# Post-norm decoder layer on one core: where in the queue the next block's feed-forward reads are issued

## The chip, the cores and the metric

The kernel runs on one core of one Trainium2 chip. The metric is device time in microseconds (us) of one execution; lower is better. A run's time includes a little that lies outside the profiled span of instructions.

The core has five engines that run side by side, each on its own stream of instructions: TensorE (PE: matmuls; its weight loads are shown apart as PEld), VectorE (DVE), ScalarE (ACT), GpSimd (POOL) and SyncE (SP), which in this kernel does nothing but issue transfers (DMAs). Transfers issued by SP, ACT or POOL are carried out by the core's 16 DMA engines.

## What is computed

The reference is one decoder layer on 8 sequences of 256 tokens, 512 wide, in float32. Cut to what matters:

```python
def reference(x, ctx_2048, Wq, Wk, Wv, Wo, Wdown, Wup, decay, gate_cp, up_cp, down_cp):
    x = layernorm(x + attention(x, ...))           # 16 heads of 32
    x = layernorm(x + xattn(x, ctx, ctx, decay))   # a decayed running sum of ctx*ctx, times x
    x = layernorm(x + ffn(x, gate_cp, up_cp, down_cp))

def ffn(h, gate_cp, up_cp, down_cp):
    gate_w = spline_reconstruct(gate_cp, 2048, 512)
    up_w   = spline_reconstruct(up_cp, 2048, 512)
    down_w = spline_reconstruct(down_cp, 512, 2048)
    inter = silu(h @ gate_w.T) * (h @ up_w.T)
    return inter @ down_w.T
```

`spline_reconstruct` makes each weight matrix by cubic interpolation of a line of control points, some 129 weights to a point. So along a row of a weight matrix the values are one cubic polynomial for a long stretch, and the kernel never builds the full matrices.

## The kernel before

**Attention and the second norm** come first, in four groups of 512 tokens, and fill the span up to about 402 us. They leave the layer's middle result in the tile `x2`.

**The feed-forward** works on four blocks `b` of 512 tokens (loop at line 939). Because a weight row is piecewise cubic, a product with it needs only two things of a token: some samples of its features near the places where the cubic changes, and a few moments (sums against fixed polynomials) for the rest. For block `b` these stand in one tile, `xgs[b]` (name `xg`, two buffers): in each half of its partitions 44 rows of samples and 20 rows of moments, for 8 places.

`inputs(b)` (line 700) makes that tile, as a generator of eight steps which `fill(n)` advances:

- Steps 1 to 4, one for each chunk `c` of 128 features: PE transposes the chunk of `x2`, ACT or DVE copies it from PSUM to the tile `xt`, and two transfers write it to a scratch tensor `xd` in device memory, in an order in which rows that are read together are near each other: the bulk from POOL's queue (line 713), and for `c` above 0 a few left-over rows from SP's queue (line 716).
- Step 5: `windows` (line 683) is called. It issues, on SP, one small write of the left-over rows of chunk 0 into `xd` (line 687) and then four reads of samples from `xd` into `xg` (line 692), two of 88 KB and two of 616 KB.
- Steps 5 to 8: PE makes the moments, DVE and ACT copy them out, POOL's queue writes them to the scratch tensor `md`, and `moments` (line 694) issues two reads of 320 KB on SP, from `md` into `xg`.

For blocks 0 and 1 (`b > 1` is false at lines 718 and 743) `inputs` runs during the last group of attention and the reads are issued at once. For blocks 2 and 3 the two calls are put into the list `reads`. `inputs(2)` is advanced in block 1 and `inputs(3)` in block 2: four steps ahead of the block's loop (line 942), the other four after the third pair (line 950).

**One block's main loop** (line 943) goes over eight pairs `j`. `gate_up` makes two tiles of 128 gate and up products from `xgs[b]`, applies silu and multiplies them into two tiles `inter`. `gather` (line 858) issues for each of them one transfer of 256 KB on SP, which regroups the rows into the tile `nat` (two halves: the first eight gatherings fill one, the last eight the other). So a block has 16 gatherings.

After the loop, block by block: the list `reads` is emptied, which issues its reads behind the 16 gatherings; then PE makes the products `y` with `exact(b, t)`, `t` from 0 to 15, four matmuls each, one for each quarter of the outputs. In this loop `slot()` advances the chains of the preceding block's third norm, whose results go out as four writes `out` on SP. At `t == 7`, `into_sums` (line 875) makes four sums `ps_s` from both halves of `nat`; each is copied out and written by SP into the tile `fin` (line 892). After `t == 15`, `finish` (line 894) adds the products of `fin` to `y`.

The order of work is written out by hand: the class `Ordered` keeps every engine's instructions in the order of the program, and since it records all operations through one helper, nearly all carry line 308 in the profile. An engine takes its instructions strictly in that order, SP among them: while SP's next transfer waits for its data, everything after it on SP waits as well. The transfers of SP share a ring of eight semaphores, used in turn.

Of the kernel before, what the change touches and what calls it, by code (L numbers as in the profile page):

```python
# [18 lines left out]
B, T, D = 8, 256, 512  # L19
# [9 lines left out]
ND = 4  # L29
# [5 lines left out]
STEP, SPAN = 8, 129  # L35
# [280 lines left out]
def decoder_kernel(ctx: ExitStack, tc: tile.TileContext, x, xT, ctxT, wq, wkT, wvT, woT, wdownT, wup, decay, up_taps, down_taps, mom_f, sum_f, out, plan):  # L316
    nc = tc.nc
# [27 lines left out]
    nc = Ordered(tc)  # L345
    units, chains = [], []

    def slot():

        for c in list(chains):  # L350
            if next(c, c) is c:
                chains.remove(c)

    def fill(n):

        for i in range(n):
            if units:
                next(units[0][1])
                units[0][2] -= 1
                if not units[0][2]:  # L360
                    units.pop(0)
            if i % 2:
                slot()
                some_taps()
# [76 lines left out]
    def some_taps():  # L441
        made[0] += 0.62
        while made[0] >= 1:
            made[0] -= 1
            next(weights, None)
# [235 lines left out]
    xgs, reads = {}, []  # L681

    def windows(xd, xt, xg):


        past = SPAN * ND - D
        nc.sync.dma_start(out=xd[4 * (SPAN - past) + 3 :: 4, :], in_=xt[:past, 0, :])
        for h, odd, n, j0 in ((0, 0, NTILE // 2 - 1, 1), (1, NTILE - 1, NTILE // 2 - 1, 0)):
            for t, m, j in ((odd, 1, odd // 2), (2 * j0 + h, n, j0)):
                step = 4 * (lows[t + 2][0] - lows[t][0]) if m > 1 else 0  # L690
                from_ = bass.AP(xd.tensor, xd.offset + 4 * lows[t][0] * GT, [[GT, RAW], [step * GT, m], [1, GT]])
                nc.sync.dma_start(out=xg[h * K2 : h * K2 + RAW, j : j + m, :], in_=from_)

    def moments(md, xg):
        for h in range(2):
            to = h * K2 + RAW
            from_ = bass.AP(md.tensor, md.offset + h * GT, [[NTILE * GT, 20], [2 * GT, NTILE // 2], [1, GT]])
            nc.sync.dma_start(out=xg[to : to + 20], in_=from_)

    def inputs(b):  # L700

        pool, mf = ffn["pool"], ffn["mf"]
        xt = pool.tile([P, DC, GT], F32, tag="x2T", name="x2T")
        xd = ffn["dram"].tile([4 * SPAN, GT], F32, tag="xd", name="xd")
        md = ffn["dram"].tile([1, 20 * NTILE, GT], F32, tag="md", name="md")
        xg = pool.tile([P, NTILE // 2, GT], F32, tag="xg", name="xg", bufs=2)
        xgs[b] = xg
        for c in range(DC):
            tr = ps_mm.tile([P, GT], F32, tag="mm", name="tr_x2")
            for t in range(TC):  # L710
                nc.tensor.transpose(tr[:, t * P : (t + 1) * P], x2[:, b * TC + t, c * P : (c + 1) * P], ident)
            (nc.vector.tensor_copy if c % 2 else nc.scalar.copy)(xt[:, c, :], tr)
            nc.gpsimd.dma_start(out=xd[c : 4 * (P - 1 - c) + c + 1 : 4, :], in_=xt[c:, c, :])
            if c:
                row = 4 * (SPAN - c) + c - 1
                nc.sync.dma_start(out=xd[row : row + 4 * c - 3 : 4, :], in_=xt[:c, c, :])
            yield
        if b > 1:
            reads.append(lambda: windows(xd, xt, xg))
        else:  # L720
            windows(xd, xt, xg)
        mo = ffn["mom"].tile([P, ND, GT], F32, tag="fin", name="mom")
        ps = {}
        for c in range(DC):
            for s in (c, c + 1):
                if s // 2 not in ps:
                    ps[s // 2] = ps_mm.tile([P, GT], F32, tag="mm", name="ps_mom")
                at = slice(s % 2 * K2, (s % 2 + 1) * K2)
                nc.tensor.matmul(
                    ps[s // 2][at, :],  # L730
                    lhsT=mf[:, c, s - c, :],
                    rhs=xt[:, c, :],
                    start=(s == c + 1 or c == 0),
                    stop=(s == c or c == DC - 1),
                )
            if c == 1:
                nc.vector.tensor_copy(mo[:, 0, :], ps[0])
            if c == DC - 1:
                nc.vector.tensor_copy(mo[:, 1, :], ps[1])
                nc.scalar.copy(mo[:K2, 2, :], ps[2][:K2, :])  # L740
                nc.gpsimd.dma_start(out=md[:, : 2 * P].rearrange("h (c p) t -> (h p) c t", p=P), in_=mo[:, :2, :])
                nc.gpsimd.dma_start(out=md[0, 2 * P :], in_=mo[:K2, 2, :])
                if b > 1:
                    reads.append(lambda: moments(md, xg))
                else:
                    moments(md, xg)
            yield
# [94 lines left out]
    def gate_up(b, j):  # L842

        pgs, pus = [], []
        for w, pool, tag, to in ((wg, ps_mm, "mm", pgs), (wu, ps_big, "big", pus)):
            for h in range(2):
                at = slice(h * K2, (h + 1) * K2)
                ps = pool.tile([P, GT], F32, tag=tag, name="pg" if w is wg else "pu")
                nc.tensor.matmul(ps, lhsT=w[at, j * P : (j + 1) * P], rhs=xgs[b][at, j, :], start=True, stop=True)
                to.append(ps)  # L850
        for h in range(2):
            sg = work.tile([P, GT], F32, tag="sg", name="sg")
            nc.scalar.activation(sg, pgs[h], AF.Silu)
            inter = work.tile([P, GT], F32, tag="inter", name="inter", bufs=NTILE)
            nc.vector.tensor_tensor(inter, pus[h], sg, ALU.mult)
            inters[b, 2 * j + h] = inter

    def gather(b, t):

        g, r = t // NSUM, t % NSUM  # L860
        if not r:
            nats[b, g] = work.tile([P, NSUM, GT], F32, tag=f"nat{g}", name="nat", bufs=1)
        nc.sync.dma_start(out=nats[b, g][r::NSUM], in_=inters[b, t])

    def exact(b, t):

        if t == 0:
            ys[b] = [ps_big.tile([P, GT], F32, tag="big", name=f"y{d}") for d in range(ND)]
        for d in range(ND):
            q = slice(d * 32, (d + 1) * 32)  # L870
            nc.tensor.matmul(
                ys[b][d], lhsT=wd[q, t * P : (t + 1) * P], rhs=inters[b, t][q, :], start=(t == 0), stop=False
            )
# [33 lines left out]
    def outcome(b, t):  # L907

        tr = ps_mm.tile([P, D], F32, tag="mm", name="tr_y")
        for d in range(ND):  # L910
            nc.tensor.transpose(tr[:, d * P : (d + 1) * P], ys[b][:, d, t * P : (t + 1) * P], ident)
        yield
        h3 = rows.tile([P, D], F32, tag="row", name="h3")
        s3 = small.tile([P, 1], F32, tag="s3", name="s3")
        nc.vector.scalar_tensor_tensor(h3, tr, 1.0, xps[b][:, t, :], ALU.mult, ALU.add, accum_out=s3)
        yield from norm_plain(h3, s3, h3, tr)
        r0 = (b * TC + t) * P
        nc.sync.dma_start(out=out[r0 : r0 + P, :], in_=h3)
# [16 lines left out]
    def settle():  # L935
        while chains:
            slot()

    for b in range(NG):
        if 0 < b < NG - 1:  # L940
            units.append(["i", inputs(b + 1), 2 * DC])
            fill(DC)
        for j in range(NTILE // 2):
            gate_up(b, j)
            gather(b, 2 * j)
            gather(b, 2 * j + 1)
            if b:
                slot()
            if b and j == 2:
                fill(DC)  # L950
        if b == 0:
            fill(2 * DC)
        while reads:
            reads.pop(0)()
        for t in range(NTILE):
            exact(b, t)
            if b and t == 0:
                chains += [outcome(b - 1, c) for c in range(TC)]
            slot()
            if b == 0 and t < 5:  # L960
                slot()
            if b == 0 and t == 4:
                settle()
                done.close()
                late = ffn["mom"] = ctx.enter_context(tc.tile_pool(name="late", bufs=1, side="right"))
            if t == 7:
                settle()
                chains.append(residual(b))
                for v in range(NSUM // 2):
                    into_sums(b, v)  # L970
        assert not units
        finish(b)
# [54 lines left out]
```

## Time and profile before

| | us |
|---|---|
| median of three runs | 616.04 (615.62 to 616.34) |
| profiled execution | 616.05 |
| its span, first to last instruction | 614.3 |
| PE busy (matmuls) | 582.3 (95%) |
| DVE / ACT / POOL busy | 334.7 / 277.7 / 210.6 |
| feed-forward, block 1: start of the next block's transposes, to the same in block 2 | 449.86 to 505.42 |
| the same, block 2 (to the first product of block 3) | 505.42 to 561.00 |
| mean granted clock of PE | 0.986 |

Times in the feed-forward are given from the start of the span. The profile's page divides the span into 40 slices and gives busy shares in tenths; "PEclk" is the granted clock of PE in tenths. In lists of instructions a group such as `xg<-xd` names what is written and what is read. "SPq" marks transfers by the time of their issue on SP; when a transfer lands is told by its semaphore's events in the trace. In a table of stretches the columns are: the stretch, its length, the busy time of PE, PEld, DVE, ACT and POOL (with the number of instructions), then the granted clock, the mean busy share of the 16 DMA engines, and GB/s. That share can come out over 1 because packets of one engine overlap. Float32 matmuls appear as two instructions each.

### The profile page before, as it was taken

Reading aid. Unit: us, or ns where it says so; the run is one execution under the profiler, and the core shown is the slowest. Engines: PE = TensorE matmul, PEld = TensorE weight load, DVE = VectorE, ACT = ScalarE, POOL = GpSimd, SP = SyncE. Lnnn points to the kernel's source line nnn. Section 1 sums busy time; section 2 is a strip of 40 time slices with the busy share of each in tenths; the row PEclk is TensorE's granted clock in tenths of the full one; section 3 lists DMA queues with packets and bytes.
Section 4 is the critical chain, followed back from the end, with each engine's and each line's share of the span. In section 5 each row is a group of like instructions: output and inputs, shape, how many; then the busy total and the mean of one; then the engine's idle time right before and its main releaser. Section 6 shows DMA issues by size and latency. Waiting matters only on the chain.

```text
span 614.3 us, 9693 instructions
## 1 busy us (share of the span) xinstructions
PE 582.3 (95%) x3346; PEld 293.8 (48%) x3346; DVE 334.7 (54%) x742; ACT 277.7 (45%) x820; POOL 210.6 (34%) x479
## 2 busy tenths in 40 slices
PE   8999999998999999999999998999999969988994
PEld 3544555555455546555546554544344334433432
DVE  0203545657875656785656778777446216503714
ACT  0115634647555447555446666563135115303502
POOL 0001986264635434635321202202611602430152
PEclk9999999999999999999999999999999979997998
DMA  8104263044224115314102654687159839982941
GB/s 286 65 0 154 85 191 104 1 138 137 56 66 138 41 47 181 112 52 138 35 18 61 187 123 126 155 200 147 71 138 229 190 104 234 197 221 59 212 151 68
DMA packets 39984, 75.50 MB, mean 123 GB/s; under 512 B 3936, under 2 KB 8288, under 8 KB 39936
## 3 DMA queue, kind: packets, MB, share of 16 engines
q1 hardware_dynamic: 36880, 66.94, 40.7%
q0 software_dynamic: 2048, 6.77, 3.4%
q10 hardware_dynamic: 1008, 1.18, 0.6%
q8 instruction: 26, 0.43, 0.3%
q14 instruction: 22, 0.18, 0.1%
HBM read 42.86 MB, written 11.04 MB: 88 GB/s over the span
## 4 chain that ended last, share of the span: by engine, by line
PE 74%; DVE 10%; DMA 9%; ACT 3%; issue 2%; SPq 1%; POOLq 0%; POOL 0%; DVEq 0%; ACTq 0%
PE ps_k L308 9%; PE ps_v L308 9%; PE y L308 8%; PE ps_o L308 8%; PE ps_q L308 7%; PE tr_e L308 6%; PE sc L308 5%; PE pg L308 5%; PE av L308 5%; DMA xg<-md 4%; PE pu L308 4%; DVE nmax L308 3%; DMA xd<-x2T 2%; PE ps_s L308 2%; PE ps_mom L308 2%; ACT e L308 2%
## 5 line engine op out<-in xcount | busy, mean ns | idle before, releaser
L308 ACT ACTIVATE e<-sc,nmax 128x256 f32<-128x256 f32 x256 | 120.0, 480 | 101.1 <-DVE nmax L308 101.1
L308 DVE TENSOR_REDUCE nmax<-sc 128x2 f32<-128x512 f32 x128 | 84.5, 682 | 73.5 <-PE sc L308 67.5
L308 POOL TENSOR_TENSOR taps<-taps 128x256 f32<-128x256 f32 (+1 forms) x144 | 88.5, 614 | 32.9 <-DMA taps<-in_down_taps 25.7
L308 PEld LDWEIGHTS tr_e<-ident,e 128*128 128x128 f32 x512 | 56.9, 140 | 25.2 <-issue 22.5
L308 PE MATMUL tr_e<-ident,e 128*128 128x128 f32 x512 | 68.3, 276 | 0.5 <-DVE eT L308 0.4
L308 PE MATMUL y<-inter,wd 32*128 32x512 f32 x512 | 63.1, 598 | 0.0
L308 POOL TENSOR_SCALAR va<-ss 128x1 f32<-128x1 f32 x32 | 7.3, 227 | 162.1 <-ACT x L308 85.8
L308 PE MATMUL ps_o<-w_o,yT 128*128 128x512 f32 x128 | 60.0, 600 | 1.6 <-DVE eT L308 1.2
L308 PE MATMUL ps_k<-xT_g,w_k 128*128 128x512 f32 x128 | 58.8, 600 | 0.7 <-DVE eT L308 0.5
L308 PE MATMUL ps_v<-w_v,xT_g 128*128 128x512 f32 x128 | 58.6, 598 | 0.4 <-DVE eT L308 0.4
L308 PE MATMUL ps_q<-xT_g,w_q 128*128 128x512 f32 x128 | 58.3, 596 | 0.0
L308 ACT ACTIVATION_READ_ACCUMULATOR e<-sc,nmax 128x1 f32 x256 | 53.2, 208 | 0.0
L308 POOL TENSOR_TENSOR rs<-va,neghalf 128x1 f32<-128x1 f32 x48 | 28.9, 602 | 69.8 <-DVE va L308 67.1
L308 DVE TENSOR_TENSOR inter<-pu,sg 128x512 f32<-128x512 f32 x64 | 41.2, 686 | 18.3 <-PE pu L308 12.4
L308 ACT ACTIVATE sg<-pg 128x512 f32<-128x512 f32 x64 | 37.3, 597 | 18.4 <-PE pg L308 18.4
L308 DVE COPY eT<-tr_e 128x512 f32<-128x512 f32 x64 | 43.7, 683 | 0.5 <-PE tr_e L308 0.4
L308 PEld LDWEIGHTS y<-inter,wd 32*128 32x128 f32 x512 | 26.7, 184 | 32.7 <-issue 26.9
L308 PE MATMUL av<-eT,v_g 128*32 128x256 f32 x512 | 36.7, 385 | 5.0 <-ACT eT L308 2.7
L308 ACT COPY eT<-tr_e 128x512 f32<-128x512 f32 x64 | 37.4, 585 | 2.4 <-PE tr_e L308 2.4
L308 PE MATMUL sc<-k_g,q_g 32*128 32x256 f32 x512 | 37.4, 401 | 0.2 <-ACT e L308 0.2
L308 POOL TENSOR_TENSOR r<-r 128x1024 f32<-128x1024 f32 x8 | 15.2, 1896 | 63.9 <-DMA r<-in_ctxT 63.9
L308 PEld LDWEIGHTS ps_v<-w_v,xT_g 128*128 128x128 f32 x128 | 23.1, 190 | 25.5 <-issue 24.3
(97 smaller groups left out, 734.8 us busy)
## 6 DMA issues: line engine op xcount, KB each, us to landing
nat<-inter SPq DMA_DIRECT2D x64, 256.0 KB
taps<-in_down_taps SPq DMA_DIRECT2D x40, 256.0 KB
taps<-in_up_taps SPq DMA_DIRECT2D x16, 384.0 KB
xg<-xd SPq DMA_DIRECT2D x8, 616.0 KB
r<-in_ctxT SPq DMA_DIRECT2D x8, 512.0 KB
x_t<-in_x SPq DMA_DIRECT2D x16, 256.0 KB
fin<-sum SPq DMA_DIRECT2D x16, 256.0 KB
out<-h SPq DMA_DIRECT2D x16, 256.0 KB
```

Of the source, the lines that this page charges most:

```text
L308: return lambda *a, **k: self.tc.keep_in_program_order(f(*a, **k))
```

## The change

Two things move; nothing is added or removed.

- The small write of chunk 0's left-over rows into `xd` goes from the start of `windows` to the first step of `inputs`, right after POOL's write of that chunk. This holds for all blocks.
- In the main loop, after the gatherings of the fourth pair (`j == 3`), the first entry of `reads` (the four reads of samples) is issued, and after those of the seventh pair (`j == 6`) the second (the two reads of moments). Before, both followed the eighth pair. Only blocks 1 and 2 have entries in `reads`.

```diff
     def windows(xd, xt, xg):
 
-
-        past = SPAN * ND - D
-        nc.sync.dma_start(out=xd[4 * (SPAN - past) + 3 :: 4, :], in_=xt[:past, 0, :])
         for h, odd, n, j0 in ((0, 0, NTILE // 2 - 1, 1), (1, NTILE - 1, NTILE // 2 - 1, 0)):
...
             nc.gpsimd.dma_start(out=xd[c : 4 * (P - 1 - c) + c + 1 : 4, :], in_=xt[c:, c, :])
+            if not c:
+
+                past = SPAN * ND - D
+                nc.sync.dma_start(out=xd[4 * (SPAN - past) + 3 :: 4, :], in_=xt[:past, 0, :])
             if c:
...
             if b and j == 2:
                 fill(DC)
+            if j in (3, 6) and reads:
+                reads.pop(0)()
         if b == 0:
             fill(2 * DC)
-        while reads:
-            reads.pop(0)()
         for t in range(NTILE):
             exact(b, t)
```

## The prediction

> **What bounds the kernel now.** I read the page's slices first, then the chain of work that ended last, the waits of PE in the feed-forward, SyncE's (SP's) queue there, and the DMA share by stretch.
>
> ```profile
> PE   8999999998999999999999998999999969988994
> PEclk9999999999999999999999999999999979997998
> DMA  8104263044224115314102654687159839982941
> PE 74%; DVE 10%; DMA 9%; ACT 3%; issue 2%; SPq 1%; POOLq 0%; POOL 0%; DVEq 0%; ACTq 0%
> ```
>
> PE sets the pace nearly everywhere (a slice is 15.36 us). The dips in the clock near the right end are in the feed-forward of blocks 1 and 2, the only blocks whose reads the change moves. There the chain leaves PE:
>
> ```profile
> 469.57 0.70 DVE inter L308
> 471.53 7.47 DMA xd<-x2T
> 479.85 0.82 SPq L308
> 480.71 13.20 DMA xg<-md
> 493.97 4.96 DMA fin<-sum
> 499.07 6.51 PE y L308 x8
> ...
> 536.32 14.12 DMA xg<-md
> 550.50 4.77 DMA fin<-sum
> 555.41 5.65 PE y L308 x8
> ```
>
> Columns: start, duration, what. In block 1 the last product (y from fin) starts at 499.07, because the fin writes were issued and served behind the reads for block 2 (xg). PE's waits in this stage say the same:
>
> ```profile
> PE y L308 <- DMA fin<-sum: 10.4, 2, 5.6
> ```
>
> 10.4 us over two blocks, 4.82 and 5.58 in the timeline of PE. The clock then falls to half, and the eight instructions take 6.51 and 5.65 us; at full clock they take 3.43 (8 x 0.429, the spacing of their weight loads in block 0). So the stalls cost 3.08 and 2.22 us more. **All that a perfect hiding of the reads could win is 4.82 + 3.08 + 5.58 + 2.22 = 15.7 us.**
>
> Next: is there room in the DMA engines where the reads are to go?
>
> ```profile
> 454.49 16.99 SPq L308 DMA_DIRECT2D nat<-inter  x16
> 471.53 0.48 SPq L308 DMA_DIRECT2D xd<-x2T  x1
> 472.19 7.55 SPq L308 DMA_DIRECT2D xg<-xd  x4
> 479.85 1.63 SPq L308 DMA_DIRECT2D xg<-md  x2
> 481.58 3.19 SPq L308 DMA_DIRECT2D out<-h  x4
> 485.14 9.36 SPq L308 DMA_DIRECT2D fin<-sum  x4
> ...
> 466.40:479.90 13.50, 13.50 (x96) 6.46 (x92) 8.87 (x22) 5.59 (x13) 4.59 (x15) 1.00 1.02 204
> 479.90:493.90 14.00, 14.00 (x100) 5.39 (x96) 1.38 (x2) 1.17 (x2) 6.96 (x31) 1.00 0.86 201
> 566.00:584.00 18.00, 18.00 (x110) 8.67 (x112) 12.56 (x28) 9.90 (x20) 3.26 (x8) 1.00 1.07 215
> ```
>
> The upper part is SP's order of issue in block 1; the lower lists stretches, with the clock, DMA share and GB/s last. While the gatherings (nat) are served the DMA share is 1.02: no room. Block 3 (the third stretch) has no reads at all and still shows 1.07. There the trace's landing events give the last gathering at 586.18, while the products that read it (ps_s) started at 585.60. In block 1 it landed at 479.90 and ps_s started at 480.08; in block 2 at 534.66 and 535.66. So the gatherings end just in time today, each taking 1.25 us of the queue (landings of 471.32, 472.59 and so on), against an issue every 1.06 us.
>
> **The change, part by part.**
>
> *The small write into xd* (four rows, 8 KB) moves from ahead of the reads to behind the first transposed chunk, in every block. Same instruction count. Today the third read waits for it: it lands at 471.53 + 7.47 = 479.00, behind the queued gatherings. Moved, it is issued near 451.4 with its three siblings, which land 0.9 to 2.3 us after issue. That takes away an SP wait of 5.4 us, but the queue held the second read meanwhile (landed 484.38) and was never empty, so I book 0. In blocks 0 and 1's inputs, made during attention, it makes SP wait for one ScalarE copy earlier, with xd writes due a few us later behind it, and the reads land at 366.68 and 401.85 at the latest against a first use at 401.7 and after 449.86: 0, bounds -0.5 to +0.5.
>
> *The four reads of samples (xg from xd)* go ahead of gatherings 9 to 16, and *the two reads of moments (xg from md)* ahead of gatherings 15 and 16. They pass nothing on POOL's queue. Their own waits are over: the last xd write landed at 457.00, and SP reaches the reads at 464.7; md landed at 466.46, and SP reaches those after 470. SP also issues a transfer only when the eighth before it has landed (a fin went at 485.14, just after an xg read landed at 485.08); behind such a wait stand the gatherings, the out writes and the fin writes. With eight in flight, some 10 us of work, the queue does not run dry, so this costs 0 by itself.
>
> What it costs is the order. In block 1 the six reads were served from 479.90 (last gathering) to 493.91 (last read), 14.0 us: landings at 480.57, 484.38, 485.08, 489.36, 491.96, 493.91, one behind the other. In block 2 it was 534.66 to 550.44, 15.8 us. In the new order the same work stands ahead of the last gathering, so that lands where the last read landed: 493.91 and 550.44.
>
> PE then works through the first four of the 32 ps_s instructions (first half of the sums; 7.02/32 = 0.219 each) until 480.08 + 0.88 = 480.96, and 536.54 in block 2, and waits: 493.91 - 480.96 = 12.95 us, and 550.44 - 536.54 = 13.90 us. What stands behind on PE are the other 28 sums, 64 y instructions (7.0 us) that need no gathering but come later in order, and the last product.
>
> The fin stall goes. The reads are done, out is served right behind the last gathering, and a fin alone lands 1.84 us after its issue (block 3, 588.75 to 590.59) under 7.0 us of y. The half clock stays: idle of 4.8 and 5.6 us caused it, idle of 13 us will too. I keep its 3.08 and 2.22 (bounds 0 and 3.41 each, half of the 6.83 us for which a record shows the clock at 0.5).
>
> Sum: block 1, 12.95 - 4.82 = +8.1; block 2, 13.90 - 5.58 = +8.3; the rest 0. +16.4 on a profiled execution of 616.05 us (span 614.3, 1.75 around it; median of the runs 616.04, so no correction): **632.5 us**.
>
> The unshown part is how reads and gatherings share the queue when mixed. Lower bound: gatherings behind the reads go at the spacing of the fin landings in block 1 (496.93, 497.61, 498.30, 498.93: 0.65 us) and not 1.25, which saves 8 x 0.6 = 4.8 a block: 622.9. Upper bound: reads at the pace they had during attention (616 KB in 4.96 and 5.0 us instead of 3.8 and 4.3, the second moments in 3.4 instead of 2.0 to 3.0), some 4 us more a block: 640. I take the middle row, since the same transfers in the same stage are nearest.
>
> Two places of the Trainium skill bear on it. The page "DMA: Bandwidth & Descriptors", section "Rules for kernel authors", advises issuing a transfer early, computing, and waiting late; by that rule alone the change wins its 15.7 us and gives 600.4. The same page, section "Why a DMA increments its semaphore by 16 and not by 1", speaks against it: a transfer uses only as many engines (at most 16) as divide its outer sizes, the lowest-numbered ones, so 44 and 20 partitions go to 11 and 10 engines, the same ones each time. With the load spread over all 16 the reads would cost about 14.9 x 10.7/16 = 10 us a block (an estimate from that page and the mean of 14.0 and 15.8) and the time would be 623; the six landings one behind the other agree with the page, not with the spread.
>
> **Rivals.**
>
> *The reads hide.* If the gatherings' 1.25 us is not engine time but waiting at their destination (a fin of the same size takes 0.65), reads could slip into those gaps. Then both stalls vanish: 616.05 - 15.7 = 600.4. It decides once the last gathering of block 1 lands before 485.8 (480.96 and the 4.82 us of idle that stand there now), so is late by less than 5.9 us and not 14. For it: the 0.65. Against: a share of 1.02 to 1.07, and reads that ran at 150 to 160 GB/s with no gathering beside them. Chance 0.10.
>
> *The gatherings catch up* behind the reads, as in the lower bound: about 619 to 625. For it: some engines are free of reads (the first piece of an out write landed at 483.57, ten microseconds before the reads ended) and will have done their share. Against: the engines that serve the reads still have all of theirs to do. Chance 0.16.
>
> *The two effects balance* within the noise: 616. Needs the last gathering to be just about 6 us late. Chance 0.03.
>
> *SP falls behind*: the wait for the eighth transfer before leaves the queue dry between reads, late gatherings delay the out writes and these the fin writes, so that a fin stall of some 5 us stays beside the new one: 632.5 + 10 = 642. Against: eight transfers in flight. Chance 0.06.
>
> *Main case*, 627 to 639: 0.65. The likeliest gives 632.5. The range 621 to 639 takes in most of the catching up and leaves out the hidden reads, the balance and the dry queue. About 0.2% (1.2 us) is what a measurement tells from no change here. Slower 0.65 + 0.16 + 0.06 = 0.87, same 0.03, faster 0.10.
>
> **What would show it.** Right: PE idle 13 us in each of blocks 1 and 2 between the fourth and fifth ps_s instruction, put down to nat; no wait of y for fin; half clock right after the idle time; SP's xg reads issued near 465 and 475; block 3 unchanged in length. Wrong: last gathering landing before 486 in block 1, ps_s running through without a wait, or y still waiting for fin.

## The result and the profile after

The changed kernel takes 631.93 us (median of four runs, 631.19 to 633.52), the kernel before 615.83 on the same chips: a ratio of 1.0266, 95% interval 1.0242 to 1.029, so some 16 us slower. The profiled execution is the slowest of the four: 633.52 us, with a span of 631.8, 17.5 longer than before.

Its slices first, then a row of its groups of instructions (busy time and mean ns; idle time of PE just before them and what ended it):

```profile
PE   8999999999999999999998988999994699569994
PEclk9999999999999999999999999999998699869998
L308 PE MATMUL ps_s<-nat,sf 128*64 128x512 f32 x128 | 34.3, 691 | 27.0 <-DMA out<-h 27.0
```

The two dips of PE are deeper than before, and the idle time has moved: 27.0 us ahead of the sums `ps_s`, where there was none, and no wait of `y` for fin any more (10.4 us before). PE in the order of time shows where in block 1 and block 2:

```profile
479.94 1.08 PE L308 MATMUL ps_s<-nat,sf 128*64 128x512 f32 x4
494.49 8.81 PE L308 MATMUL ps_s<-nat,sf 128*64 128x512 f32 x28 [13.47 <-DMA out<-h]
503.24 7.15 PE L308 MATMUL y<-inter,wd 32*128 32x512 f32 x64
510.31 3.70 PE L308 MATMUL y<-fin,wd 128*128 128x512 f32 x8
513.85 1.91 PE L308 MATMUL tr_x<-ident,x 128*128 128x128 f32 x16
...
544.09 1.08 PE L308 MATMUL ps_s<-nat,sf 128*64 128x512 f32 x4
558.67 9.15 PE L308 MATMUL ps_s<-nat,sf 128*64 128x512 f32 x28 [13.49 <-DMA out<-h]
567.75 7.15 PE L308 MATMUL y<-inter,wd 32*128 32x512 f32 x64
574.83 3.70 PE L308 MATMUL y<-fin,wd 128*128 128x512 f32 x8
```

Four instructions of the sums, then 13.5 us of nothing, then the other 28, in 8.81 and 9.15 us instead of the 6.23 that they take at full clock (shown below, with the moments alone). The last product follows the others without a wait. The bracket names an out write, and that is a slip of the profile, which guesses the releaser from semaphores that transfers share: these sums read only `nat` and a constant. The landing events decide: the sixteenth gathering landed at 494.30, just before PE went on at 494.49; the first out write landed later, at 494.97.

SP's order of issue in block 1 of the changed kernel:

```profile
454.35 10.12 SPq L308 DMA_DIRECT2D nat<-inter  x8
464.65 2.40 SPq L308 DMA_DIRECT2D xg<-xd  x4
467.15 7.33 SPq L308 DMA_DIRECT2D nat<-inter  x6
474.79 6.67 SPq L308 DMA_DIRECT2D xg<-md  x2
481.97 1.83 SPq L308 DMA_DIRECT2D nat<-inter  x2
484.35 4.00 SPq L308 DMA_DIRECT2D out<-h  x4
497.11 7.48 SPq L308 DMA_DIRECT2D fin<-sum  x4
```

The reads are issued where the change puts them, 7.5 and 5.1 us sooner than before. But the last gathering lands 14.4 us later, at 494.30 and not at 479.90.

From the transposes of one block's inputs to the next mark, block 1 now takes 64.1 us (55.6 before) and block 2 64.6 (55.6): +8.6 and +9.0. Everything else is as it was: block 3, from its first product to the end of the span, takes 53.3 us in both.

### The profile page after: what moved, and what is told of

The parts are those of the page before. It is cut to its first block, busy times and chain, and to the rows that moved or that the text cites. A ratio compares the mean times of both kernels' runs of the same rounds, so it can differ in the third digit from the quotient of the medians.

```text
span 631.8 us, 9694 instructions
## 1 busy us (share of the span) xinstructions
PE 582.7 (92%) x3346; PEld 293.3 (46%) x3346; DVE 334.9 (53%) x742; ACT 277.9 (44%) x820; POOL 210.1 (33%) x479
## 4 chain that ended last, share of the span: by engine, by line
PE 77%; DVE 10%; DMA 9%; ACT 3%; issue 1%; POOLq 0%; POOL 0%; SPq 0%; DVEq 0%; ACTq 0%
PE y L308 9%; PE ps_k L308 9%; PE ps_v L308 9%; PE ps_o L308 8%; PE ps_q L308 7%; PE tr_e L308 6%; PE ps_s L308 5%; DMA nat<-inter 5%; PE sc L308 5%; PE pg L308 5%; PE av L308 4%; PE pu L308 4%; DMA out<-h 3%; DVE nmax L308 3%; PE ps_mom L308 2%; ACT e L308 2%
## 5 line engine op out<-in xcount | busy, mean ns | idle before, releaser
L308 PE MATMUL ps_s<-nat,sf 128*64 128x512 f32 x128 | 34.3, 691 | 27.0 <-DMA out<-h 27.0
L308 POOL TENSOR_TENSOR r<-r 128x1024 f32<-128x1024 f32 x8 | 15.2, 1896 | 63.9 <-DMA r<-in_ctxT 63.9
```

Source lines behind the costliest of these rows:

```text
L308: return lambda *a, **k: self.tc.keep_in_program_order(f(*a, **k))
```

## The experiments

The theory is that of the prediction: transfers of SP are served in the order of issue, and whatever stands ahead of the last gathering delays it by its own time of service. The rivals: SP itself, held by its ring of eight semaphores; reads that hinder each gathering after them; the small write. Ten kernels were run, each beside the kernel before on the same chip.

**The small write alone.** The reads are issued after the loop again:

```diff
-            if j in (3, 6) and reads:
-                reads.pop(0)()
         if b == 0:
             fill(2 * DC)
+        while reads:
+            reads.pop(0)()
```

> Only the small write into xd moves; the six reads stay behind the sixteenth gathering. Theory (order in the DMA queue): 616, within 1.5 us of before: SP's 5.4 us wait for that write goes, but the queue was never empty meanwhile, so the last read still lands at about 494 and y still waits some 5 us for fin in blocks 1 and 2. Rival (that wait is what made fin late): the reads end some 5 us sooner, the fin wait falls to about nothing, 601 to 606.

Measured: 615.07 against 615.96, ratio 0.9992 (0.9979 to 1.0005). The last read lands at 493.87 (493.91 before), and `y` still waits 10.4 us for fin in the two blocks. The move of the small write is worth nothing: SP's wait for it was covered by the read in service.

**Only the samples, or only the moments, among the gatherings.** The first keeps `if j == 3` with the rest after the loop, the second `if j == 6 and reads: reads.pop(1)()` with the rest after the loop.

> The four sample reads stand behind the fourth pair as in the change, the two moment reads behind the sixteenth gathering as before. Theory: the last gathering lands later by the samples' service alone, 9.5 to 10.5 us, so PE is idle some 8.5 us ahead of the fifth ps_s instruction, no wait for fin: +3 us a block, 622 (619 to 625). Rival (reads slow every gathering that comes after them, most of the price is theirs for standing so early): as the change, 630 or more.

> The two moment reads stand behind the seventh pair as in the change, the four sample reads behind the sixteenth gathering as before. Theory: the last gathering is late by 4.5 to 5.5 us, which costs PE 3.5 to 4.5 us of idle time ahead of the fifth ps_s instruction; the fin writes stand behind 9.5 us of sample reads, but PE gets to y from fin later too, so the wait there is under 1 us: faster than before, 610 (605 to 614). Rival (SP's ring of eight semaphores: SP is held for 5 us ahead of the second moment read and so issues the last two gatherings late): slower than before, 620 or more.

Measured: samples alone 626.27 (ratio 1.0173, 1.015 to 1.0196), above the theory's 619 to 625 and below the rival's 630. Moments alone 610.00 (ratio 0.991, 0.9885 to 0.9935): faster than before, as the theory had it, where the rival had 620 or more. PE in block 1 with the moments alone:

```profile
479.49 1.08 PE L308 MATMUL ps_s<-nat,sf 128*64 128x512 f32 x4
483.35 6.23 PE L308 MATMUL ps_s<-nat,sf 128*64 128x512 f32 x28 [2.77 <-DMA nat<-inter]
...
497.58 3.67 PE L308 MATMUL y<-fin,wd 128*128 128x512 f32 x8 [0.93 <-DMA fin<-sum]
```

PE is idle for 2.77 and 0.93 us, and the clock stays up; in block 2 it is idle for 3.73 us, not at all for fin, and the half clock costs 1.7 us (7.92 us for the 28 sums). Here the same rule works in the kernel's favour: two short reads ahead of the last gathering cost little there, and 4.5 us of service no longer stand ahead of fin. So "reads among the gatherings" is neither good nor bad; it is a matter of how many microseconds of service are put ahead of which deadline.

With the samples alone the idle time was 9.8 and 10.7 us, not the 8.5 expected. The landings tell why: the two 616 KB reads of block 1, which take 3.8 and 4.3 us behind the gatherings, took 4.4 and 6.3 while gatherings were served beside them on the engines that they leave free.

**The place among the gatherings.** All six reads behind the seventh pair: `while j == 6 and reads: reads.pop(0)()`.

> All six reads stand behind the seventh pair, so two gatherings follow them and not eight. Theory: the place among the gatherings does not matter, only that the last one stands behind the reads: last gathering near 494, idle of 13 us, as the change within 3 us: 632. Rival (reads hinder the gatherings that follow, one by one): two instead of eight are hindered, a quarter to a half of the loss, 619 to 624.

Measured: 628.95 (ratio 1.0218, 1.0194 to 1.0242), idle of 11.5 and 11.8 us:

```profile
PE ps_s L308 <- DMA nat<-inter: 23.3, 2, 11.8
```

With two gatherings behind the reads instead of eight, four fifths of the loss remain (13.0 of 16.1 us). So the order against the last gathering makes the loss; hindering gatherings one by one would have left half or less. The fifth that goes fits the slowing of the reads just seen: here the large ones took 4.0 and 4.2 us in block 1, and all six 14.2 us, against 16.6 with the change.

**Another queue for the reads.** As the change, with the reads of blocks 2 and 3 issued by GpSimd, on a ring and semaphores of its own (`b_` is the block that the reads are for):

```diff
-                nc.sync.dma_start(out=xg[h * K2 : h * K2 + RAW, j : j + m, :], in_=from_)
+                (nc.gpsimd if b_ > 1 else nc.sync).dma_start(out=xg[h * K2 : h * K2 + RAW, j : j + m, :], in_=from_)
...
-            nc.sync.dma_start(out=xg[to : to + 20], in_=from_)
+            (nc.gpsimd if b_ > 1 else nc.sync).dma_start(out=xg[to : to + 20], in_=from_)
```

> As the change, but the six reads of blocks 2 and 3 are issued on POOL's queue, with semaphores of its own, so SP is never held by them. Theory (engine time): reads and gatherings still share the same DMA engines in the same stretch, so the last gathering is late by most of the reads' service: it lands at 487 to 494, time 618 to 632. Rival (SP's ring of semaphores, or being behind in one ring): SP issues the gatherings as before, the last lands by 482, no stall of ps_s and none of fin: 600 to 605.

Measured: 625.89 (ratio 1.0156, 1.013 to 1.0181), so 9.3 of the 16.1 us of loss remain. PE at the fifth instruction of the sums, in blocks 1 and 2:

```profile
493.18 8.75 PE L308 MATMUL ps_s<-nat,sf 128*64 128x512 f32 x28 [11.11 <-DMA out<-h]
552.99 7.86 PE L308 MATMUL ps_s<-nat,sf 128*64 128x512 f32 x28 [9.20 <-DMA nat<-inter]
```

In block 1 SP was no longer held by the reads and issued its last gathering by 476.9, against 483.8 with the change; the gathering landed at 492.94 all the same. So SP's semaphores are not what makes most of the loss, and the place of the reads in SP's ring isn't needed for it either: two rings share the same 16 engines, and the gatherings between them come out nearly as late. Why the other 6 to 7 us went is not shown: this run changes SP's holding, the order between the two rings and the way in which GpSimd issues transfers all at once.

**Splitting the large reads.** As the change, each 616 KB read in two, of 32 and of 12 rows.

```diff
+                for r, k in ((0, 32), (32, 12)) if m > 1 else ((0, RAW),):
...
+                    from_ = bass.AP(xd.tensor, at, [[GT, k], [step * GT, m], [1, GT]])
+                    nc.sync.dma_start(out=xg[h * K2 + r : h * K2 + r + k, j : j + m, :], in_=from_)
```

> As the change, but each of the two 616 KB sample reads goes in two, of 32 and of 12 rows. Theory (the page DMA: Bandwidth & Descriptors has 44 rows on 11 engines, 32 on 16 and 12 on 12): the busiest engines carry 21 pieces of 2 KB in place of 28 for each, some 1 us less for each read, so the last gathering lands some 2 us sooner and the time is 627 to 629. Rival (bytes in all count, or more transfers cost more): 632 or above.

Measured: 635.94 (ratio 1.0326, 1.0295 to 1.0357), slower than the change, and the theory's detail falls: the semaphores of the two parts step 16 and 12 times as their pieces land, the counts of engines that were expected, yet the samples of block 1 were served in 11.9 us, from 469.80 to 481.69, against 11.3 with the change. More engines did not help.

**What sets the pace of a read.** Two kernels with the reads behind the sixteenth gathering, where they are served without gatherings beside them. In one, the bytes of a 616 KB read come from one stretch of `xd`; in the other, four reads fill the whole tile on all 128 partitions:

```diff
+                if b_ > 1 and m > 1:
+                    from_ = bass.AP(xd.tensor, xd.offset + 64 * h * GT, [[m * GT, RAW], [GT, m], [1, GT]])
```

```diff
+    def whole(xd, xg):
+        for j in range(0, NTILE // 2, 2):
+            from_ = bass.AP(xd.tensor, xd.offset + 32 * j * GT, [[GT, P], [P * GT, 2], [1, GT]])
+            nc.sync.dma_start(out=xg[:, j : j + 2, :], in_=from_)
```

> Reads behind the sixteenth gathering. In blocks 2 and 3 each 616 KB read takes its bytes from one unbroken stretch of xd, 14 KB for each partition, and not from seven places 128 KB apart; same 44 partitions, same bytes, so the samples are not the reference's. It asks what sets the 3.8 to 4.3 us of such a read. If the places read in device memory do: 2.5 us or less, fin wait gone, about 604 to 608. If the 44 written partitions or the share of the DMA engines used do: 3.8 to 4.3 us as before, 615.

> Reads behind the sixteenth gathering. In blocks 2 and 3 four reads of 512 KB into all 128 partitions replace the four sample reads and the two moment reads: the same 2 MB into the same tile, but samples and moments are not the reference's. If the number of partitions (44 and 20, and the engines that go with them) sets the pace of the reads: 2 MB in 7 us or less in place of 14, fin no longer waits, 600 to 605. If the bytes do: 14 us again, 615.

Measured: from one stretch 614.72 (ratio 0.9989, 0.9976 to 1.0002), the two reads still 4.0 and 3.9 us. On all partitions 600.39 (ratio 0.9751, 0.9728 to 0.9774). The stretch in which the reads are served, on the kernel with the small write alone and then on this one:

```profile
480.20:493.90 13.70, 13.70 (x98) 5.33 (x96) 1.38 (x2) 1.17 (x2) 6.71 (x30) 1.00 0.84 200
```

```profile
480.10:485.20 5.10, 5.10 (x28) 1.73 (x26) 0.69 (x1) 0.59 (x1) 5.10 (x24) 1.00 1.05 393
```

The columns are those of the table of stretches before. Two megabytes in 5.1 us at 393 GB/s, against 13.7 us (the 200 GB/s there include out and fin writes on engines that the reads leave free). So neither the bytes nor, for the samples, the places read in device memory set the pace, but the shape at the tile: 44 and 20 adjacent partitions at a time. The trace's packets show two parts of it. Fewer engines seem to work: as the pieces land, the semaphore of a sample read steps 11 times and that of a moment read 10 times, the counts of engines that the prediction gives, against 16 on all partitions. And each piece is slow: with one stretch, a piece of 14 KB took 1.10 us (median of 176), or 157 ns for 2 KB, while a piece of 2 KB on all partitions took 85 ns.

The number of partitions alone is not the measure, though: a fin write puts 256 KB into 32 partitions, every fourth one, and takes 0.65 us of a full queue (some 400 GB/s, from the tile `sum`). Whether it matters which partitions are written together was not varied for the reads. The split into 32 and 12 rows, which brought in the other engines and gained nothing, speaks against the engines as the only cause, but was measured among gatherings.

**A version that beats both.** The theory says what to do: put ahead of each deadline only what it needs. The gatherings are wanted first (480), then fin (494), then the reads (about 499). So the samples stay behind the sixteenth gathering and the moments go behind the fin writes:

```diff
-            if j in (3, 6) and reads:
-                reads.pop(0)()
         if b == 0:
             fill(2 * DC)
+        if reads:
+            reads.pop(0)()
...
                 for v in range(NSUM // 2):
                     into_sums(b, v)
+                if reads:
+                    reads.pop(0)()
```

> Small write early, sample reads behind the sixteenth gathering, moment reads behind the fin writes. Theory: the gatherings end at 480 as before, so ps_s waits for nothing; sample reads (to about 490), out and fin writes are served by about 494.5, when PE ends its y products, so the wait for fin is 0 to 1 us and the clock stays up; the moments land near 499, when the next block's first products want them: 602 (599 to 607), faster than both kernels. Rival (SP's ring of eight semaphores delays fin: its fourth waits for the fourth sample read): fin wait of 3 us or more with half clock, 609 to 616.

Measured: 603.07 (ratio 0.979, 0.9771 to 0.981). Fin comes 1.32 and 1.02 us late, not more. The next step holds back the four out writes, which nothing waits for, until after the moments: `outcome` appends its write to a list, emptied behind the reads above (in the last block it goes out at once).

> As the kernel with the moment reads behind the fin writes, and the out writes of the third norm are issued behind those too. Theory: fin, which still came 1.3 and 1.0 us late there, no longer stands behind 2.5 us of out writes, lands near 492, and y waits for nothing: 2 to 2.5 us faster than that kernel, 600.5 to 601.5, a ratio to before of 0.974 to 0.977. Rival (fin is late because its fourth waits in SP for the fourth sample read): 603 as that kernel.

Measured: 600.98 us (median of five runs, 600.47 to 601.30), ratio 0.9761 (0.9745 to 0.9777). SP in its block 1, then PE in blocks 1 and 2:

```profile
471.75 3.75 SPq L308 DMA_DIRECT2D xg<-xd  x4
482.78 5.79 SPq L308 DMA_DIRECT2D fin<-sum  x4
488.62 1.66 SPq L308 DMA_DIRECT2D xg<-md  x2
490.32 2.37 SPq L308 DMA_DIRECT2D out<-h  x4
```

```profile
480.19 7.09 PE L308 MATMUL ps_s<-nat,sf 128*64 128x512 f32 x32
494.28 3.70 PE L308 MATMUL y<-fin,wd 128*128 128x512 f32 x8
497.82 1.91 PE L308 MATMUL tr_x<-ident,x 128*128 128x128 f32 x16
542.16 3.70 PE L308 MATMUL y<-fin,wd 128*128 128x512 f32 x8
```

All 32 sums run in one piece, and the last product starts with no bracket behind it and takes 3.70 us, as at full clock. The fin writes land by 492.24, the moments by 496.92, the out writes by 499.45. This is 31 us less than the changed kernel and 14.6 less than the kernel before beside it, of the 15.2 that perfect hiding could win (worked out below). The all-partition reads, at 600.39 in the old order, suggest that quicker reads would add little to it.

## Why the prediction was right

The forecast was 632.5, the measurement 631.93: slower, and by the mechanism named. Step by step:

- *What could be won at most*, 15.7 us: right but for half a microsecond. The eight instructions of the last product were read as 6.51 and 5.65 us from the timeline, to the end of the last one, against 3.43 from their spacing alone. By the timeline they take 3.70 at full clock (510.31 above), so the half clock cost 2.8 and 2.0 us and not 3.08 and 2.22, and the sum is 15.2. The version that puts every transfer ahead of its deadline won 14.6 us (615.55 - 600.98), the one with quick reads 15.2.
- *No room among the gatherings*: right. It was read from a DMA share of 1.02 to 1.07 and from gatherings that landed 0.2 us (block 1) and 1.0 us (block 2) ahead of their use. The moments alone, the samples alone and both together show PE's idle time growing with the service put ahead of the last gathering: some 3, 10 and 13.5 us.
- *Where the last gathering lands*, 493.91 and 550.44 in the old time: 494.30 in block 1. In block 2, where everything starts 8.4 us later, 558.43, or 550.0 in the old time.
- *PE's idle time*, 12.95 and 13.90 us at the fifth instruction of the sums: 13.47 and 13.49.
- *No wait for fin*: right; a fin alone landed 1.8 us after its issue, as in block 3 before.
- *The half clock*, 3.08 and 2.22 kept: 2.6 and 2.9, from 8.81 and 9.15 us against 6.23. With the 2.8 and 2.0 before on the same measure, block 1 pays 0.2 less and block 2 1.0 more, where the sum has no change.
- *The small write and SP's ring of semaphores*, booked at 0: for the small write the first experiment shows it. For the ring, GpSimd's queue shows that most of the loss is there without it, not that it costs nothing. SP was in fact held, ahead of the second moment read (issued at 480.70) and of the last two gatherings, but the queue went on working: the DMA share was 0.95 from 464.7 to 480 and 0.83 from 480 to 494.

The landing time came out better than its parts. The service of the reads was taken from where they run behind the gatherings; among them the six take 16.6 us in block 1 and not 14.0, the two large ones 4.5 and 6.0 and not 3.8 and 4.3. On the other side the last eight gatherings took 8.9 us and not 11.1, the very last two 0.95 and 0.64: the rival in which the gatherings catch up is there, with 2.2 of the 4.8 us that it reckoned. The two misses nearly cancel, and the 0.4 us left over is luck of that kind. So is the nearness of the total: the profiled execution grew by 17.5 us against 16.4 in the sum, while the medians differ by 16.1.

The estimate beside the sum, that the reads would cost 10 us if spread over all 16 engines, found no support: the samples, spread by rows, cost as much, and on all 128 partitions the same bytes cost 5.1. Nor do landings one behind the other tell how many engines serve a read, as the prediction had it: the four reads on all partitions land so too. The advice of "Rules for kernel authors" on the Trainium skill's page "DMA: Bandwidth & Descriptors", to issue a transfer early, did not hold here for reads that went out at 464.65 and 474.79, are used past 510, and had gatherings behind them that were due at 481.

## What to carry to other kernels

In this kernel a full queue finished its large transfers in the order in which they were issued, so moving one forward moved all that it passed back by about its time of service. Sort transfers by when their data is wanted, not by when it is there. Before moving a read into a busy stretch, look at whether the DMA share there is at 1 and at how long before its use the last transfer of that stretch lands now. A wait that shows up at one place (fin) can be paid for by the transfers with no deadline: here the moments and the out writes.

## What was not expected of the hardware

- Reads into 44 and 20 adjacent partitions are slow. In the kernel before, 616 KB into 44 partitions took 3.8 to 4.4 us (143 to 166 GB/s), 320 KB into 20 partitions 2.0 to 3.0; 512 KB into 128 partitions, in the kernel made for it, took 1.35 (some 390 GB/s). With 14 KB pieces in place of 2 KB pieces the large samples took the same, 4.0 and 3.9.
- The same read is slower beside gatherings: 5.4 to 6.3 us for the second large one (the change and the samples alone), 4.3 in the kernel before.
- The half clock does not keep to PE's idle time. In the changed kernel the trace's clock records show it for 13.65 and 17.07 us, though PE was idle for 13.5 us both times; in the kernel before they show 6.83 in either block. With the change it begins 5.1 and 2.4 us into the idle time and ends 5.2 and 5.9 us after PE has gone on. Half of those last stretches, 2.6 and 3.0 us, is about what the sums lost. With the moments alone, 2.77 us of idle time passed without it and 3.73 did not.
